# Counting the slots of a mixture of experts on TensorE, and moving one combining add to ScalarE and GpSimd, in a four-layer kernel

## The chip, the core and the metric

The kernel runs on one core of one Trainium2 chip. The metric is the device time of one execution in microseconds (us). The engines are called PE (TensorE), DVE (VectorE), ACT (ScalarE), POOL (GpSimd) and SP (SyncE), as in the profile.

## The reference

The input x is 32 sequences of 64 rows of 512 numbers, 2048 rows in all. Four layers follow one another, each of the form x = x + f(cond(x)). Only the first two matter here.

```python
x = x + L0_ffn(L0_cond(x, ...))      # attention, one shared expert, 7 routed experts of which each row takes 2
x = x + L1_ffn(L1_cond(x, ...))      # 32 routed experts of which each row takes 4
x = x + L2_ffn(L2_cond(x, ...))      # soft mixture of 16 experts
x = x + L3_ffn(L3_cond(x, ...))      # attention over a block cache, int8 product
# a routed layer:
topk, idx = top_k(x @ router, K)
y = sum over the K chosen experts e of  weight[e] * expert_e(x)
```

All is in single precision (fp32), except where small whole numbers are handled.

## The kernel before

**Tiling.** The rows are cut into 16 tiles (`NT`) of 128 rows, one row for each partition. A routed layer (class `Moe`, once with E0 = 7 experts, K0 = 2 choices and C0 = 640 slots an expert, once with E1 = 32, K1 = 4 and C1 = 320) works in three parts.

1. *Routing*, tile by tile. `choose` takes the logits of a tile and leaves the best values and their indices (`max`, `max_index`). `put` gives each chosen (row, expert) pair a slot, for n tiles at a time. It makes one-hot rows `hot` (n x K x E numbers a partition), sums them over K into `sel`, and keeps running sums over the tiles in `pre`, whose first entry holds each expert's first slot, e x C, divided by 128. Two matrix products into the PSUM tile `at` give each row the number of pairs ahead of it: a matrix of ones times `pre` adds over the 128 rows of all earlier tiles, and a strictly upper triangular matrix times `sel` adds over the earlier rows of the same tile. `hot` times `at`, summed over the experts, is the slot. `mark` then writes the row numbers into a table by slot: two comparisons on DVE make 16-bit one-hot matrices `a_` and `b_`, ACT scales `a_` by the row number, PE multiplies them, and DVE adds the product to `tokens`. After the last tile `end` casts it to `stok`, and compares the totals with C.
2. *Experts*. `ready` and `rows_of` gather the rows by `stok` with an indirect DMA issued from POOL (`xr`), and `run` multiplies unit by unit of 320 slots. The results go to the scratch tensor `ys`.
3. *Combining*, done by the layer that follows. `combined` gathers a row's K results (`yk`, an indirect DMA from POOL) and adds each, times its weight `gates`, to x with one DVE instruction. Layer 1 combines the two results of layer 0 in this way, layer 2 the four of layer 1.

**Layer 0's front** is class `Front`: thirteen stages in an order written out by hand (`turns`), four tiles in flight. Every second step `down` calls `put` for two tiles, the last two are counted in `gate_up`. `at` is a slice of the PSUM bank that `tok` and the router's logits also use.

**Layer 1's front** is the loop over 16 tiles in `layer1`: combine into `x1in`, multiply by the condition's weights on PE (`mm`), copy to `c` on ACT, write `c` to `rows` with a DMA from SP, transpose on PE (`tp`), copy to `cT` on ACT, multiply by the router on PE (`rp`), add its bias on DVE (`lg`), and choose. `put` is called for tiles 0 to 3, 4 to 7, 8 to 11, 12 and 13, 14, and 15, each one tile late. Here `at` has a bank of its own.

**Order.** Each engine runs its instructions in the order in which they stand in its queue. A scheduler makes that order, by dependences and expected times, except for those that `keep_in_program_order` pins; nothing in the parts changed here is pinned. An engine waits at the head of its queue, so what stands behind waits too.

The lines that the change and the prediction touch:

- L284 `gather`: every indirect DMA on POOL (`yk`, `xr`)
- L743 `hot`, L748 `sel`, L750 `pre`, L753 and L754 the two products, L755 `hot` times `at`, L757 its sum `sl`
- L719 the comparisons of `mark`, L725 ACT's scaling of `a_`, L727 PE's products, L728 the sum `tokens`
- L767 `stok`, L772 and L773 the totals
- L970 the combining add, L1056 `mm`, L1058 `c`, L1064 `cT`, L1067 `rp`, L1069 `lg`

`yk` has six buffers in layer 1, so a gather waits until the add of three tiles before has read its buffer.

Of the kernel before, what the change touches and what calls it, by code (L numbers as in the profile page):

```python
# [9 lines left out]
F32 = mybir.dt.float32  # L10
BF16 = mybir.dt.bfloat16
# [3 lines left out]
AF = mybir.ActivationFunctionType  # L15
ALU = mybir.AluOpType
AX = mybir.AxisListType
# [3 lines left out]
P = 128  # L21
B, T, D = 32, 64, 512
NT = B * T // P
# [5 lines left out]
E0, K0, C0, V0 = 7, 2, 640, 24  # L29
# [151 lines left out]
class Prog:  # L181


    def __init__(self, tc, a, ctx):
        self.tc, self.nc, self.a = tc, tc.nc, a
        self.const = ctx.enter_context(tc.tile_pool(name="const", bufs=1))
        self.dram = ctx.enter_context(tc.tile_pool(name="scratch", bufs=1, space=DRAM))
        self.named = {}
        self.constants(self.const, "cst")
        self.flip = 0  # L190
        self.ident = self.c("ident")
        self.ones = self.c("ones")
# [470 lines left out]
class Moe:  # L663
# [7 lines left out]
    def __init__(self, g, ctx, keep, E, K, C, V, wname, wlen, act, scale):  # L671
        self.g, self.keep, self.E, self.K, self.C, self.V = g, keep, E, K, C, V
        self.wname, self.wlen, self.act, self.scale = wname, wlen, act, scale
        tc = g.tc
        self.tiles = E * C // P
        self.rows = g.stream(f"rows{E}")
        self.ys = g.ys[E]
        self.slot = g.const.tile([P, NT, K], I32, name=f"slot{E}")
        self.gates = g.const.tile([P, NT, K], F32, name=f"gates{E}")
        self.vals = keep.tile([P, NT, 8], F32, name=f"vals{E}")  # L680
        self.chosen = keep.tile([P, NT, K], F32, name=f"chosen{E}")
        self.place = keep.tile([P, NT, K], F32, name=f"place{E}")
        self.idx = keep.tile([P, NT, 8], U32, name=f"idx{E}")

        self.pre = keep.tile([P, NT + 1, E], F32, name=f"pre{E}")
        self.count = keep.tile([P, E], F32, name=f"count{E}")
        self.stok = keep.tile([P, self.tiles], I32, name=f"stok{E}")
        self.wp = ctx.enter_context(tc.tile_pool(name=f"ew{E}", bufs=3, reuse_waits="tile"))
        self.wts = {}
# [8 lines left out]
    def begin(self, sb, bank, at):  # L698
        nc, iota = self.g.nc, self.g.c("iota")[:, 0 : self.E]
        self.bank, self.at = bank, at  # L700
        nc.vector.tensor_scalar(self.pre[:, 0], iota, self.C / P, None, ALU.mult)
        self.tok = sb.tile([P, self.tiles], F32, name="tokens", bufs=1)
        nc.vector.memset(self.tok, 0.0)

# [31 lines left out]
    def put(self, sb, i, n):  # L736

        g, nc, E, K, C = self.g, self.g.nc, self.E, self.K, self.C
        fi, place = self.chosen[:, i : i + n, :], self.place[:, i : i + n, :]
        nc.vector.tensor_copy(fi, self.idx[:, i : i + n, 0:K])  # L740
        shape = [P, n, K, E]
        hot = sb.tile(shape, F32, name=f"hot{n}", bufs=1)
        nc.vector.tensor_tensor(  # L743
            hot, g.c("iota")[:, 0:E].unsqueeze(1).unsqueeze(1).to_broadcast(shape),
            fi.unsqueeze(3).to_broadcast(shape), ALU.is_equal,
        )
        sel = sb.tile([P, n, E], F32, name=f"sel{n}")
        nc.vector.tensor_reduce(sel, hot.rearrange("p n k e -> p n e k"), AX.X, ALU.add)  # L748
        for j in range(n):
            nc.vector.tensor_tensor(self.pre[:, i + j + 1], self.pre[:, i + j], sel[:, j], ALU.add)  # L750

        at = self.at[:, 0 : n * E].rearrange("p (n e) -> p n e", n=n)
        nc.tensor.matmul(at, g.ones, self.pre[:, i : i + n], start=True, stop=False)  # L753
        nc.tensor.matmul(at, g.c("upper"), sel, start=False, stop=True)  # L754
        nc.vector.tensor_tensor(hot, hot, at.unsqueeze(2).to_broadcast(shape), ALU.mult)  # L755
        sl = sb.tile([P, n, K], F32, name=f"sl{n}")
        nc.vector.tensor_reduce(sl, hot, AX.X, ALU.add)  # L757
        slot = self.slot[:, i : i + n, :]
        nc.vector.tensor_copy(slot, sl)
        nc.vector.scalar_tensor_tensor(place, fi, -float(C), sl, ALU.mult, ALU.add)  # L760
        ov = sb.tile([P, n, K], F32, name=f"ov{n}")
        nc.vector.tensor_scalar(ov, place, float(C), BIG, ALU.is_ge, ALU.mult)
        self.mark(sb, self.bank[:, 0 : self.tiles], self.tok, sl, slot, ov, i, n, self.tiles)

    def end(self, sb):
        g, nc, E, C = self.g, self.g.nc, self.E, self.C
        nc.vector.tensor_copy(self.stok, self.tok)  # L767

        lim = sb.tile([P, E], F32, name="lim")
        nc.vector.tensor_scalar(lim, g.c("iota")[:, 0:E], float(C), float(C), ALU.mult, ALU.add)  # L770
        tot = self.at[:, 0:E]
        nc.tensor.matmul(tot, g.ones, self.pre[:, NT], start=True, stop=True)  # L772
        nc.vector.tensor_tensor(self.count, tot, lim, ALU.subtract)  # L773
        nc.vector.tensor_scalar(self.count, self.count, 0.0, None, ALU.max)

    def ready(self, ctx):
# [10 lines left out]
    def beyond(self):  # L787
# [10 lines left out]
        with tc.If(n > 0), ExitStack() as ctx:  # L798
# [10 lines left out]
            nc.vector.memset(zero, 0.0)  # L809
            end = sb.tile([P, E], F32, name="end")  # L810
            nc.vector.tensor_tensor_scan(end, tf, zero, 0.0, ALU.add, ALU.add)
            start = sb.tile([P, E], F32, name="start")
            nc.vector.tensor_tensor(start, end, tf, ALU.subtract)
            nc.vector.tensor_scalar(start, start, float(P), -float(self.C), ALU.mult, ALU.add)
            stok = sb.tile([P, V], I32, name="vtok")
# [61 lines left out]
    def run(self, xs, per_tile):  # L877

        g, nc, tc, E, K, C = self.g, self.g.nc, self.g.tc, self.E, self.K, self.C
        units = E * C // UNIT  # L880
        with ExitStack() as ctx:
            sb = ctx.enter_context(tc.tile_pool(name=f"es{E}", bufs=3, reuse_waits="tile"))
# [57 lines left out]
            for u in range(units):  # L940
                p = u // 2
# [20 lines left out]
        def combined(pool, i, bufs, x=None, out=None):  # L962
            if x is None:
                x = g.load_x(pool, xs, i, bufs)
            if out is None:
                out = x
            for k in range(K):
                yk = pool.tile([P, D], F32, name="yk", bufs=4 if K == K1 else 6)
                g.gather(yk, self.ys, self.slot[:, i, k : k + 1])
                nc.vector.scalar_tensor_tensor(out, yk, self.gates[:, i, k : k + 1], x, ALU.mult, ALU.add)  # L970
                x = out
            return out

# [1121 lines left out]
```

## Time and profile before

| | us |
|---|---|
| median of 3 runs | 2802.5 (2797.17 to 2808.08) |
| the profiled execution | 2786.42 |
| its span, first to last instruction | 2784.6 |
| PE busy in the span | 2567.1 (92%) |
| DVE busy | 1404.6 (50%) |
| ACT busy | 748.2 (27%) |
| POOL busy | 846.8 (30%) |

The profile is of one execution. "Busy" is the time in which an engine had an instruction at work; matmuls overlap, so that a busy PE is not PE at its peak. The stages follow each other in the span: layer 0's front up to about 422 us, its experts up to about 645, layer 1's front from 655 to 744, its experts up to about 1260, then layers 2 and 3. A row of a group reads: line, engine, operation, tile written and tiles read, shapes, count, then busy time and mean of one in ns, then the engine's idle time just before them and what ended it. A row of the timeline reads: start, duration, engine, line, operation, and in brackets the idle time before it with what ended that.

### The profile page before, as it was taken

How to read it: one execution, taken by the hardware profiler on the slowest of the kernel's cores; microseconds unless marked ns; L12 is line 12 of the kernel's file. 1: busy time of each engine (PE TensorE's matmuls, PEld its weight loads, DVE VectorE, ACT ScalarE, POOL GpSimd, SP SyncE). 2: the span in 40 equal slices, each digit the busy share in tenths (PEclk: the TensorE clock that was granted, in tenths of full speed). 3: DMA queues.
4: the chain of work that ended last, by engine and by line, in shares of the span. 5: the costliest groups of instructions: out<-in, count | busy, mean ns of one | idle time of the engine just before them, and what ended most of it. 6: DMA issues, size and time to landing. Idle time of an engine off the chain costs nothing.

```text
span 2784.6 us, 42002 instructions
## 1 busy us (share of the span) xinstructions
PE 2567.1 (92%) x16556; PEld 1640.1 (59%) x16571; DVE 1404.6 (50%) x3479; ACT 748.2 (27%) x1557; POOL 846.8 (30%) x904
## 2 busy tenths in 40 slices
PE   5999998997699999996899999999999999788878
PEld 4777765654555655654666666667666654344444
DVE  3666655734754333334455544445554416466656
ACT  2444430112211121111222222222222212354444
POOL 2222114624222223213122222222222108656550
PEclk9999999998699999998999999999999999889898
DMA  2233224446545965534010000001000025124340
GB/s 93 91 124 127 96 77 164 156 148 191 169 166 195 345 228 211 201 125 156 17 38 27 28 27 28 27 31 50 27 27 27 31 78 182 53 74 115 89 112 29
DMA packets 107078, 291.21 MB, mean 105 GB/s; under 512 B 20682, under 2 KB 21482, under 8 KB 99569
## 3 DMA queue, kind: packets, MB, share of 16 engines
q1 hardware_dynamic: 71232, 193.46, 19.5%
q0 software_dynamic: 35056, 89.13, 11.0%
q10 hardware_dynamic: 576, 5.77, 0.5%
q8 instruction: 135, 2.21, 0.3%
q14 instruction: 79, 0.64, 0.1%
HBM read 216.76 MB, written 87.56 MB: 109 GB/s over the span
## 4 chain that ended last, share of the span: by engine, by line
PE 48%; DVE 3%; issue 2%; POOL 1%; DMA 1%; another core or an unknown queue 1%; ACT 0%; SPq 0%; ACTq 0%; POOLq 0%; DVEq 0%
PE lp L1356 8%; PE out L1499 8%; PE zp L1433 8%; PE hp L1465 3%; PE gp L1488 2%; PE pp L1803 2%; PE y L2032 2%; PE op L2010 2%; PE sp L1963 2%; PE yp L1301 2%; PE pT L1985 2%; PE ep L1442 1%; PE kp L1936 1%; PE ap L1289 1%; PE csum L1452 1%
## 5 line engine op out<-in xcount | busy, mean ns | idle before, releaser
L910 PE MATMUL gu<-xT,wt 128*128 128x320 f32 x1472 | 407.1, 434 | 0.0
L910 PEld LDWEIGHTS gu<-xT,wt 128*128 128x128 f32 x1472 | 277.7, 191 | 119.5 <-issue 11.4
L1356 PEld LDWEIGHTS lp<-xnT,sb_mu 128*128 128x128 f32 x2048 | 235.7, 193 | 8.8 <-issue 6.7
L1356 PE MATMUL lp<-xnT,sb_mu 128*128 128x128 f32 x2048 | 238.6, 277 | 1.5 <-DVE xnT L256 0.8
L929 PE MATMUL y<-wt,hT 128*128 128x512 f32 (+1 forms) x552 | 238.7, 606 | 0.1
L1499 PE MATMUL out<-sb_w,gT 128*128 128x512 f32 x512 | 233.6, 599 | 0.0
L1433 PE MATMUL zp<-sb_w,xnT 128*128 128x512 f32 x512 | 226.5, 592 | 0.0
L1492 DVE COPY gT<-gp 128x512 f32<-128x512 f32 x64 | 44.3, 692 | 235.4 <-PE gp L1488 235.0
L284 POOL DMA_INDIRECT xr<-rows,stok x115 | 110.2, 958 | 154.7 <-PE tp L891 86.1
L1433 PEld LDWEIGHTS zp<-sb_w,xnT 128*128 128x128 f32 x512 | 93.7, 190 | 104.7 <-issue 100.9
L1499 PEld LDWEIGHTS out<-sb_w,gT 128*128 128x128 f32 x512 | 93.4, 190 | 103.5 <-issue 95.2
L929 PEld LDWEIGHTS y<-wt,hT 128*128 128x128 f32 (+1 forms) x552 | 80.0, 171 | 104.9 <-issue 88.4
L659 POOL TENSOR_TENSOR ga<-ga,sg 128x320 f32<-128x320 f32 x64 | 55.2, 863 | 283.4 <-ACT sg L655 281.3
L284 POOL DMA_INDIRECT yk<-ys,slot x96 | 99.5, 1036 | 123.9 <-SPq L798 65.2
L1510 POOL TENSOR_TENSOR xt<-xt,bc_bias 128x512 f32<-128x512 f32 x16 | 20.3, 1270 | 360.1 <-DMA x<-xt 360.1
L1470 ACT ACTIVATE h<-hp 128x512 f32<-128x512 f32 x128 | 69.5, 594 | 214.2 <-PE hp L1465 214.0
L1970 DVE CUSTOM_DVE_ANT_0 s<-sp,mask 128x336 f32<-128x336 f32 x128 | 61.4, 504 | 124.2 <-PE sp L1963 42.8
L284 POOL DMA_INDIRECT kvt<-kv,gidx x96 | 94.9, 989 | 93.6 <-PE op L2010 64.7
L1394 POOL TENSOR_TENSOR eT<-eT,inv 128x512 f32<-128x512 f32 x64 | 71.6, 1120 | 151.2 <-DVE inv L1393 149.3
L284 POOL DMA_INDIRECT kvt<-newkv,oidx x96 | 98.3, 1024 | 38.9 <-issue 29.9
L2032 PE MATMUL y<-sb_w_o,oT 128*128 128x512 f32 x128 | 74.4, 667 | 22.5 <-DVE y3s L1516 16.0
L891 PEld LDWEIGHTS tp<-sb_cst,xr 128*128 128x128 f32 x460 | 53.7, 147 | 65.4 <-issue 32.3
(379 smaller groups left out, 4616.2 us busy)
## 6 DMA issues: line engine op xcount, KB each, us to landing
wt<-w_e SPq DMA_DIRECT2D x32, 1538.0 KB
ys<-yo SPq DMA_DIRECT2D x115, 256.0 KB
ys<-zero SPq DMA_DIRECT2D x10, 2048.0 KB
xt<-x SPq DMA_DIRECT2D x62, 256.0 KB
wt<-w_e SPq DMA_DIRECT2D x7, 1536.0 KB
x<-xt SPq DMA_DIRECT2D x32, 256.0 KB
sb_w<-w SPq DMA_DIRECT2D x5, 1024.0 KB
rows<-hn SPq DMA_DIRECT2D x16, 256.0 KB
```

The lines of the kernel that those rows point to most:

```text
L284: ins = self.nc.gpsimd.indirect_dma_start(out=out, out_offset=None, in_=src, in_offset=bass.IndirectOffsetOnAxis(ap=idx, axis=0), **kw)
L910: nc.tensor.matmul(o, wj[:, c, ic * P : (ic + 1) * P], xT[:, c, :], start=c == 0, stop=c == 3)
L929: nc.tensor.matmul(y[row : row + n, :], hTs[u][:, ic, col : col + n], wd[:, ic, :], start=ic == 0, stop=ic == 1,)
L1301: g.first(c, nc.tensor.matmul(yp, self.xT[:, c, :], w["w_2"][:, c, :], start=c == 0, stop=False))
L1356: g.first(e + c, nc.tensor.matmul(lp[:, e, :], w["mu"][:, c, (4 * q + e) * P : (4 * q + e + 1) * P], self.xnT[:, c, :], start=c == 0, stop ...
L1394: g.pin(nc.gpsimd.tensor_tensor(e3, e3, inv.unsqueeze(2).to_broadcast([P, 8, T]), ALU.mult))
L1433: g.first(c, nc.tensor.matmul(zp, self.xnT[:, c, :], w["w1"][:, c, cols], start=c == 0, stop=c == 3))
L1465: g.first(e + b, nc.tensor.matmul(hp[:, b, e, :], self.ews[q][r, e, :], self.z[q][r, e * P : (e + 1) * P], start=True, stop=True))
L1470: g.pin(nc.scalar.activation(self.hs[q][b], hp[:, b], AF.Gelu))
L1499: g.first(e, nc.tensor.matmul(self.out, self.gTs[q][:, e, :], w["w2"][:, 4 * q + e, :], start=q + e == 0, stop=q + e == 6 and q == 3))
L1970: nc.vector.tensor_tensor_reduce(p, sps[j], self.masks[2 * i + half], -0.0625, 3.0e38, ALU.add, ALU.min, m)
L2032: nc.tensor.matmul(yp, self.oT[i][:, c // 2, c % 2, :], w["w_o3"][:, c, :], start=c == 0, stop=c == 3)
```

## The change

In `put`, the sums move from DVE to PE. The one-hot rows `hot` are written in bfloat16, and so are two copies of the triangular and the all-ones matrix (`masks`). `sel` and `pre` are gone. The counts in `at` are built up by 1 + K + nK products: the running base of each expert, in single precision by the identity; the triangular matrix times `hot`, for each of the K choices; and the all-ones matrix times the `hot` of each tile and choice, added to all later tiles of the call and to one further column group. ACT copies that last group to `base`, where the next call begins. The product of `hot` and `at` goes to a tile of its own, `own`. `end` takes the totals from `base` and needs no product for them.

In `combined`, for K0 = 2 choices (layer 0's results, combined in layer 1), the first add stays one DVE instruction. The second becomes two: ACT scales `yk` by the weight in place, and POOL adds it to the tile.

```diff
@@ class Moe, __init__ and begin
-        self.pre = keep.tile([P, NT + 1, E], F32, name=f"pre{E}")
+        self.base = keep.tile([P, E], F32, name=f"base{E}")
+        self.masks = keep.tile([P, 2, P], BF16, name=f"masks{E}")
...
-        nc.vector.tensor_scalar(self.pre[:, 0], iota, self.C / P, None, ALU.mult)
+        nc.vector.tensor_scalar(self.base, iota, float(self.C), None, ALU.mult)
+        for j, k in enumerate(("upper", "ones")):
+            nc.vector.tensor_copy(self.masks[:, j], self.g.c(k))
@@ put
-        hot = sb.tile(shape, F32, name=f"hot{n}", bufs=1)
+        hot = sb.tile(shape, BF16, name=f"hot{n}", bufs=1)
...
-        sel = sb.tile([P, n, E], F32, name=f"sel{n}")
-        nc.vector.tensor_reduce(sel, hot.rearrange("p n k e -> p n e k"), AX.X, ALU.add)
+        at = self.at[:, 0 : (n + 1) * E].rearrange("p (n e) -> p n e", n=n + 1)
+        nc.tensor.matmul(
+            at, g.ident, self.base.unsqueeze(1).to_broadcast([P, n + 1, E]), start=True, stop=False
+        )
+        for k in range(K):
+            nc.tensor.matmul(at[:, 0:n], self.masks[:, 0], hot[:, :, k], start=False, stop=False)
         for j in range(n):
-            nc.vector.tensor_tensor(self.pre[:, i + j + 1], self.pre[:, i + j], sel[:, j], ALU.add)
-        at = self.at[:, 0 : n * E].rearrange("p (n e) -> p n e", n=n)
-        nc.tensor.matmul(at, g.ones, self.pre[:, i : i + n], start=True, stop=False)
-        nc.tensor.matmul(at, g.c("upper"), sel, start=False, stop=True)
-        nc.vector.tensor_tensor(hot, hot, at.unsqueeze(2).to_broadcast(shape), ALU.mult)
+            for k in range(K):
+                nc.tensor.matmul(
+                    at[:, j + 1 :], self.masks[:, 1], hot[:, j : j + 1, k].to_broadcast([P, n - j, E]),
+                    start=False, stop=j == n - 1 and k == K - 1,
+                )
+        nc.scalar.copy(self.base, at[:, n])
+        own = sb.tile(shape, F32, name=f"own{n}", bufs=1)
+        nc.vector.tensor_tensor(own, hot, at[:, 0:n].unsqueeze(2).to_broadcast(shape), ALU.mult)
         sl = sb.tile([P, n, K], F32, name=f"sl{n}")
-        nc.vector.tensor_reduce(sl, hot, AX.X, ALU.add)
+        nc.vector.tensor_reduce(sl, own, AX.X, ALU.add)
@@ end
-        tot = self.at[:, 0:E]
-        nc.tensor.matmul(tot, g.ones, self.pre[:, NT], start=True, stop=True)
-        nc.vector.tensor_tensor(self.count, tot, lim, ALU.subtract)
+        nc.vector.tensor_tensor(self.count, self.base, lim, ALU.subtract)
@@ run, combined
-                nc.vector.scalar_tensor_tensor(out, yk, self.gates[:, i, k : k + 1], x, ALU.mult, ALU.add)
+                gate = self.gates[:, i, k : k + 1]
+                if K == K0 and k:
+                    nc.scalar.activation(yk, yk, AF.Copy, scale=gate)
+                    nc.gpsimd.tensor_tensor(out, out, yk, ALU.add)
+                else:
+                    nc.vector.scalar_tensor_tensor(out, yk, gate, x, ALU.mult, ALU.add)
```

## The prediction

> **What bounds the kernel now.** I read the page first, then busy time by stage, then the groups and the timeline of the one stage where both edits do most of their work.
>
> ```profile
> span 2784.6 us, 42002 instructions
> PE 2567.1 (92%) x16556; PEld 1640.1 (59%) x16571; DVE 1404.6 (50%) x3479; ACT 748.2 (27%) x1557; POOL 846.8 (30%) x904
> ```
>
> Over the whole span TensorE (PE) is the bound. The stage table (columns: stretch, its length, busy time of PE, weight loads, VectorE, ScalarE, GpSimd, then granted clock, DMA share, GB/s) shows where it is not:
>
> ```profile
> 100.00:400.00 300.00, 287.38 (x3192) 217.91 (x3191) 189.26 (x485) 121.54 (x210) 61.69 (x87) 1.00 0.31 105
> 655.00:683.00 28.00, 16.17 (x51) 9.97 (x52) 10.88 (x22) 4.62 (x9) 20.36 (x19) 0.62 0.73 212
> 683.00:714.00 31.00, 26.68 (x158) 18.91 (x157) 27.00 (x91) 12.55 (x24) 14.78 (x13) 0.87 0.63 188
> 714.00:744.00 30.00, 17.53 (x108) 13.55 (x107) 25.97 (x101) 10.22 (x19) 0.00 (x0) 0.58 0.48 190
> 755.00:1260.00 505.00, 495.27 (x1757) 286.98 (x1756) 199.16 (x410) 90.60 (x191) 126.63 (x137) 1.00 0.59 208
> ```
>
> Layer 0's front (100 to 400) and layer 1's experts (from 755) are PE at 96 to 98%. Between 655 and 744 lies layer 1's front: PE is at half clock much of the time and VectorE is busy for 53 of the 61 us after 683. GpSimd (POOL) issues 32 gathers up to 710 and then nothing. The groups of 655 to 744:
>
> ```profile
> L284 POOL DMA_INDIRECT yk<-ys,slot x32 | 35.2, 1099 | 85.7 <-SPq L798 65.2 <-DVE vals L733 10.5 <-issue 5.8
> L970 DVE SCALAR_TENSOR_TENSOR x1in<-yk,gates,x1in 128x512 f32<-128x512 f32 x16 | 11.9, 744 | 3.0 <-DMA yk<-ys,slot 2.8
> L748 DVE TENSOR_REDUCE sel<-hot 128x128 f32<-128x512 f32 x3 | 3.1, 1028 | 0.0
> L750 DVE TENSOR_TENSOR pre<-pre,sel 128x32 f32<-128x32 f32 x16 | 2.9, 184 | 0.0
> ```
>
> The last three are what the change takes from VectorE. The end of the front, in order of time:
>
> ```profile
> 722.45 0.69 DVE L755 TENSOR_TENSOR hot<-hot,at 128x512 f32<-128x512 f32 x1 [0.55 <-PE at L754]
> 724.24 0.74 DVE L970 SCALAR_TENSOR_TENSOR x1in<-yk,gates,x1in 128x512 f32<-128x512 f32 x1
> 729.19 0.59 ACT L1064 COPY cT<-tp 128x512 f32<-128x512 f32 x1 [1.26 <-PE tp L1062]
> 731.78 0.19 DVE L1069 TENSOR_TENSOR lg<-rp,bc_b_r 128x32 f32<-128x32 f32 x1 [1.23 <-PE rp L1067]
> 744.43 0.94 POOL L284 DMA_INDIRECT xr<-rows,stok  x1 [33.79 <-DVE stok L767]
> ```
>
> The last tile's second add is at 724.2, its logits at 731.8; the slots are final at 743.7, and only then can the expert rows be gathered (744.4). All that follows, PE-bound, moves with that moment.
>
> **What the Trainium skill says.** (1) "SBUF — State Buffer", Who interferes with whom: a VectorE instruction with two SBUF inputs and a GpSimd one that reads SBUF lock each other out for a whole instruction. No overlap in this trace isolates it; L1394's GpSimd multiplies do spread from 1.03 to 1.49 us. (2) "GPSIMD Engine Reference", Elementwise — side-by-side cycle accounting: a two-input add is about twice as slow there. The trace agrees: 1.27 us (L574, 128x512) against 0.74 for L970. (3) "ScalarE: Activation LUTs", What ACT_TABLE_LOAD costs: 0.83 ns an element plus a fixed part that grows by 93 ns for each per-row operand. The plain 128x512 copy is 0.59 us in the trace, so the scaled one is estimated at 0.65. (4) "TensorE: Matmul & The Clock Gate", Back-to-back issue gap: about 81 ns for a load and matmul of 128 columns. The trace agrees: 16 half-precision pairs in 1.30 us (L727 at 718.6).
>
> **The change part by part.** The sum is against the profiled execution, 2786.4 us (span 2784.6 and 1.8 around it), which is 16 below the median 2802.5 of the runs; I add the same microseconds to the median.
>
> Layer 0, eight counts of two tiles. Removed from PE: two single-precision products, four issues 0.11 us apart (112.41 to 112.74), 0.44. Added: one of them (0.22) and six 16-bit pairs at 0.08 (0.48), 0.70. So 8 x 0.26 = 2.1, minus the final total's pair (L772, 0.3): **+1.8** on a PE that is 96% busy. Ends: 0 if it all falls into PE's 4% of idling, +3. From VectorE go 0.18 + 2 x 0.18 us a count (L748, L750), worth nothing beside the busy PE. The ScalarE copy of the running base (about 0.25) is hidden likewise; the two mask copies run before the stage.
>
> Layer 1's adds. VectorE loses 16 x 0.74 = 11.9 us. ScalarE gets 16 x 0.65 = 10.4 on top of 27.4 in 89, but in its in-order queue, where each scaled copy waits for a gather to land. Behind it stand the copies `c` and `cT` (who waits: PE, then VectorE's logits) and the base copies. GpSimd gets 16 x 1.27 = 20.3 us in the queue that issues the gathers. Walk it: six gathers at 1.25 each from 655 end at 662.5. Then 26 gathers x 1.25 and 16 adds x 1.4 (1.27 and 0.13 of dispatch, estimated) are 54.9: 717.4 if it never waits. The last gather then issues at 714.8, lands 4.0 later (the first one: 654.97 to 659.07), is scaled by 719.4 and added by 720.8. That is about 4 us before the old 725.0. GpSimd, which had 13 us of waits to spare, is now the bound of this part.
>
> Layer 1's counts. VectorE loses sel (3.1 + 0.6 + 0.7) and pre (2.9): 7.3 us. PE gains 88 16-bit pairs less 7 single-precision pairs, some 5 us of a PE that is one third idle here. The new dependence is the point. In the built instruction order the multiply of hot and counts (old L755) waits for ScalarE's copy of the new base, and this copy sits in ScalarE's queue where the order puts it: for tiles 8 to 11, behind the last tile's `cT`. Walk the end: add 720.8; product 1.1 and `c` 0.6 give 722.5; ScalarE's next four instructions scale the token marks of tiles 4 to 7 (1.92): 724.4; `cT` at 725.0. From 724.1 PE works through 16 token and 20 count pairs, interleaved, 36 x 0.09 = 3.2: 727.4. Base copy 727.7. So the multiply for tiles 8 to 11 starts at 727.9, where it was 722.45. From there the old kernel took 743.5 - 722.45 = 21.0 us to the slots. Of that 2.1 us (sel, pre and the last add, by their spacing) is gone, and 1.2 of waiting for the last logits. New waits are these logits again (1.0), 12 pairs, base copy and hop for tiles 12 and 13 (0.9), the base copy behind tile 14's marks (0.5), and one hop for each base copy (1.2). 727.9 + 21.4 = 749.3: **+5.8**.
>
> The port. During 662 to 721 GpSimd adds hold it for about 20 of 59 us, and VectorE's two-input work (L970's first adds 12, the comparisons of L719 about 8, L743 2) for 22. If an add meets such work in one case of three and loses half of it (0.4 for an add, 1.1 for a 2.29 us comparison), that is about **+3**; ends 0 and +12 (every add losing 0.75). SyncE's queue gets no more and no fewer transfers; its writes of `rows` follow `c`, the expert weights behind them, and both are landed by 744. PE's clock, 0.58 to 0.87 here, may rise with more matmuls: -2 to 0, taken as 0.
>
> Sum: 1.8 + 5.8 + 3 = +10.6: 2797 for the profiled execution, **2813** on the median (+0.38%). About 0.5%, 14 us, is what a measurement of this kernel can tell from no change.
>
> **Rivals.** *GpSimd locks up the gathers (slower).* In-order adds waiting for the port delay the gathers behind them, hence the scaled copies, hence the base copies and VectorE. With adds at 1.9 and gathers at 1.5 (1.4 to 1.5 was seen on the old gathers beside L970), the queue takes 26 x 1.5 + 16 x 1.9 = 69.4 instead of 54.9: +14.5 on 1.8 + 5.8, about 2825. It passes 0.5% once adds average 1.8 us. For it: GpSimd becomes the bound with no slack; against it: the order keeps three tiles of gathers ahead. *VectorE's relief decides (faster).* VectorE is 87% busy after 683. If queue positions on ScalarE don't bind, half of the moved adds (6) and all of sel and pre (7.3) come off: -13.3 + 1.8 is -11.5, 2791; over 0.5% only if the early adds count too (-17, 2785). Against it: the walk finds ScalarE, not VectorE, last. *No effect:* the moved scaling could load a table each time (1.28 us). Between plain copies and L725's scaled ones the stage shows no load before 736.8, so I exclude it.
>
> **How the numbers follow.** The walk 0.60, mostly -3 to +18; the GpSimd lock 0.30, +14 to +30; VectorE's relief 0.10, -17 to -6. Within 0.5%: about 0.42 of the first, 0.05 of the second, 0.07 of the third, and the rest of the first lies above 14. I give 0.05 faster, 0.55 same, 0.40 slower. The range leaves out the top of the lock and the bottom of the relief: 2793 to 2832.
>
> **What would show it.** Right: no L748/L750 groups; GpSimd adds of 1.3 to 1.6 us between gathers up to about 720 to 725; the multiply for tiles 8 to 11 waiting for ScalarE at 726 to 730, after the last `cT`; first xr gather at 748 to 755; layer 0 ending 1 to 2 us later. Wrong: that gather before 744 (relief won), or after 758 with adds near 2 us (lock), or a layer 0 shifted by over 4 us.

## The result, and the profile after

The changed kernel takes 2814.73 us (median of 20 runs) beside 2804.76 us for the kernel before (20 runs): ratio 1.0034, 95% interval [1.0018, 1.0049], about 9.5 us more by the ratio. The profiled execution of it took 2813.8 us, the one of before 2786.4, which is less than the fastest of the 20 runs (2792.84). Most of that gap of 27 us is scatter: up to layer 3 the traces are only some 7 us apart, and the other 20 come up in layer 3, whose code the change doesn't touch (502 us before, 522 after, and 506 in a second trace of the same changed kernel).

In all that follows, "the stretch" is layer 1's front from the first `yk` gather to the cast of the slots to integers (`stok`). It was 88.5 us before (654.97 to 743.49) and is 91.2 us after (656.82 to 748.03). The head of the page:

```profile
span 2812.0 us, 42199 instructions
PE 2586.5 (92%) x16660; PEld 1648.7 (59%) x16675; DVE 1392.4 (50%) x3421; ACT 760.6 (27%) x1587; POOL 864.5 (31%) x920
```

VectorE (DVE) lost 12 us over the whole span and GpSimd (POOL) gained 18. The stage table, columns as before, shows where it went:

```profile
655.00:683.00 28.00, 15.03 (x54) 9.03 (x54) 7.01 (x20) 8.82 (x15) 22.21 (x22) 0.62 0.60 177
683.00:714.00 31.00, 28.41 (x163) 20.96 (x161) 18.33 (x55) 13.99 (x27) 26.24 (x22) 0.70 0.61 183
714.00:744.00 30.00, 18.99 (x168) 14.93 (x168) 26.91 (x83) 14.81 (x31) 8.59 (x6) 0.81 0.61 229
```

In the first two rows VectorE fell from 37.9 to 25.3 us of 59, and GpSimd rose from 35.1 to 48.5. The engine that had time to spare is now the full one. The groups of 655 to 744, shapes kept apart:

```profile
L284 POOL DMA_INDIRECT yk<-ys,slot x32 | 33.2, 1037 | 73.8 <-SPq L806 65.3 <-issue 5.4 <-DVE own L765 1.3
...
L982 POOL TENSOR_TENSOR x1in<-x1in,yk 128x512 f32<-128x512 f32 x16 | 23.9, 1492 | 3.7 <-ACT yk L981 3.3 <-issue 0.2
...
L984 DVE SCALAR_TENSOR_TENSOR x1in<-yk,gates,xt 128x512 f32<-128x512 f32 x16 | 13.6, 849 | 22.1 <-DMA yk<-ys,slot 22.1
L981 ACT ACTIVATE yk<-yk,gates 128x512 f32<-128x512 f32 x16 | 11.6, 722 | 25.5 <-DMA yk<-ys,slot 24.0 <-POOL x1in L982 1.5
...
L722 DVE TENSOR_TENSOR a<-sb_cst,tl 128x1280 f16<-128x1280 f32 x3 | 6.6, 2197 | 0.0
```

Two of these groups looked like this in the kernel before:

```profile
L970 DVE SCALAR_TENSOR_TENSOR x1in<-yk,gates,xt 128x512 f32<-128x512 f32 x16 | 11.9, 744 | 9.7 <-DMA yk<-ys,slot 9.7
L719 DVE TENSOR_TENSOR a<-sb_cst,tl 128x1280 f16<-128x1280 f32 x3 | 4.5, 1485 | 0.0
```

Two things are to be seen. GpSimd's own queue hardly waits: apart from the wait before the first gather (65.3) its gathers waited 8.5 us and its adds 3.7, where the old gathers waited 20.5. And three means are too high for what the instructions do. The GpSimd add averages 1.49 us although 14 of the 16 took 1.26 to 1.29; VectorE's first add averages 0.85 (15 took 0.73 to 0.75 and one 2.43), where the kernel before had 0.74; the comparison `a` of 1280 columns averages 2.20, where each of before's took 1.48. The end of the stretch, in order of time:

```profile
723.34 2.66 POOL L982 TENSOR_TENSOR x1in<-x1in,yk 128x512 f32<-128x512 f32 x1 [1.97 <-ACT yk L981]
726.06 1.12 PE L1070 MATMUL mm<-x1in,wbd 128*128 128x512 f32 x2 [1.61 <-POOL x1in L982]
727.70 1.92 ACT L728 ACTIVATE a<-a,sb_cst 128x320 f16<-128x320 f16 x4
729.52 0.57 ACT L1078 COPY cT<-tp 128x512 f32<-128x512 f32 x1
730.76 0.18 ACT L763 COPY base<-at 128x32 f32<-128x32 f32 x1 [0.67 <-PE at L759]
730.98 0.69 DVE L765 TENSOR_TENSOR own<-hot,at 128x512 f32<-128x512 bf16 x1
731.67 0.19 DVE L1083 TENSOR_TENSOR lg<-rp,bc_b_r 128x32 f32<-128x32 f32 x1
749.06 0.96 POOL L284 DMA_INDIRECT xr<-rows,stok  x1 [23.06 <-DVE gm L1112]
```

The last add takes 2.66 us, and TensorE waits for it. Behind the last tile's product stand, in TensorE's queue, that tile's transposes, another tile's logits, and then the token products and the counts of tiles 8 to 11; after these come the base copy and the multiply (L765), which starts at 730.98, where it was 722.45. This is the chain that the prediction walked, but for `cT`, which the counts don't wait for. The last logits (731.67) are where they were (731.78). The expert gather comes at 749.06 instead of 744.43. From that gather to the start of the experts' last product it is 509.2 us, 508.1 before: the experts only move.

### The profile page after: what moved, and what is told of

The parts are those of the page before. It is cut to its first block, busy times and chain, and to the rows that moved or that the text cites. A ratio compares the mean times of both kernels' runs of the same rounds, so it can differ in the third digit from the quotient of the medians.

```text
span 2812.0 us, 42199 instructions
## 1 busy us (share of the span) xinstructions
PE 2586.5 (92%) x16660; PEld 1648.7 (59%) x16675; DVE 1392.4 (50%) x3421; ACT 760.6 (27%) x1587; POOL 864.5 (31%) x920
## 3 DMA queue, kind: packets, MB, share of 16 engines
q0 software_dynamic: 35056, 89.13, 10.6%
## 4 chain that ended last, share of the span: by engine, by line
PE 47%; DVE 3%; another core or an unknown queue 2%; issue 1%; POOL 1%; ACT 1%; DMA 1%; POOLq 0%; ACTq 0%; SPq 0%; DVEq 0%
PE out L1513 8%; PE lp L1370 8%; PE zp L1447 7%; PE hp L1479 3%; PE gp L1502 2%; PE pp L1817 2%; PE y L2046 2%; PE sp L1977 2%; PE op L2024 2%; PE yp L1315 2%; PE pT L1999 2%; PE ep L1456 1%; PE kp L1950 1%; PE ap L1303 1%
## 5 line engine op out<-in xcount | busy, mean ns | idle before, releaser
L284 POOL DMA_INDIRECT yk<-ys,slot x96 | 97.6, 1017 | 112.9 <-SPq L806 65.3
L284 POOL DMA_INDIRECT kvt<-kv,gidx x96 | 93.3, 972 | 122.4 <-PE op L2024 95.7
L1988 ACT ACTIVATE s<-s,m 128x336 f32<-128x336 f32 x128 | 73.1, 574 | 80.5 <-DVE m L1984 41.1
```

Source lines behind the costliest of these rows:

```text
L284: ins = self.nc.gpsimd.indirect_dma_start(out=out, out_offset=None, in_=src, in_offset=bass.IndirectOffsetOnAxis(ap=idx, axis=0), **kw)
L1988: nc.scalar.activation(p, p, AF.Exp, bias=m, scale=-1.0, accum_out=tot)
```

## The experiments

Runs of one group shared a chip and the runs of the kernel before that belong to it; medians of before were 2792.5, 2704.6 and 2791.7 us for the three groups, so ratios are compared and not microseconds.

### Group 1: the parts alone

**adds**: only the last hunk of the change, the scaled copy on ScalarE and the sum on GpSimd; its diff is that hunk:

```diff
-                nc.vector.scalar_tensor_tensor(out, yk, self.gates[:, i, k : k + 1], x, ALU.mult, ALU.add)
+                gate = self.gates[:, i, k : k + 1]
+                if K == K0 and k:
+                    nc.scalar.activation(yk, yk, AF.Copy, scale=gate)
+                    nc.gpsimd.tensor_tensor(out, out, yk, ALU.add)
+                else:
+                    nc.vector.scalar_tensor_tensor(out, yk, gate, x, ALU.mult, ALU.add)
```

> Of the change, the moved add of layer 1 alone; counting as before. T1 (the moved add paces layer 1's front: the GpSimd order, and VectorE's two-input comparisons and GpSimd's adds blocking each other): first yk gather to first xr gather 92 to 95 us (89.5 before, 92.2 with the whole change), a GpSimd add of 2.5 us or more and a VectorE comparison of 2.5 us where they overlap, median 2808 to 2812. T2 (the counts' chain TensorE, ScalarE, VectorE paces it): front 89 to 90 us, median within 3 us of before. Both: layer 0's stok cast stays at 421.3 us.

Measured: ratio 1.0038 [1.0021, 1.0056]; stretch 98.8 us, longer than either theory had it.

**counts**: all hunks but that one.

```diff
-                if K == K0 and k:
-                    nc.scalar.activation(yk, yk, AF.Copy, scale=gate)
-                    nc.gpsimd.tensor_tensor(out, out, yk, ALU.add)
-                else:
-                    nc.vector.scalar_tensor_tensor(out, yk, gate, x, ALU.mult, ALU.add)
+                nc.vector.scalar_tensor_tensor(out, yk, gate, x, ALU.mult, ALU.add)
```

> Of the change, the counts on TensorE alone (both layers); the second add of layer 1 as before on VectorE. T1: layer 0 ends 1 to 2 us later as with the whole change (stok cast 422.5), layer 1's front takes 89.5 us or less (down to 86, since the stretch from the last large multiply to the cast was 17.1 us against 21.0), median between 3 us under and 2 us over before. T2: front 92 to 93 us as with the whole change, median 2811 to 2815.

Measured: 0.9985 [0.9974, 0.9997]; stretch 84.5 us.

**counts1** and **counts0** choose the counting by the layer (counts1 as shown; in counts0 it is `E == E0`); the first branch holds the new lines of `put`, the second the old ones:

```diff
+        self.on_pe = E == E1
...
+        if self.on_pe:
...
+        else:
+            sel = sb.tile([P, n, E], F32, name=f"sel{n}")
+            nc.vector.tensor_reduce(sel, hot.rearrange("p n k e -> p n e k"), AX.X, ALU.add)
...
```

> Of the change, the counts on TensorE in layer 1 alone; layer 0's counts and layer 1's adds as before. T1: stok cast of layer 0 at 421.3, front 86 to 89.5 us, median 0 to 5 us under before: a kernel that could beat both. T2: front 92 to 93 us, median 3 to 5 us over before.

> Of the change, the counts on TensorE in layer 0 alone. T0 (the counting products lie on TensorE's path in layer 0): stok cast 1 to 1.5 us and first yk gather 1.2 to 2.5 us later than before (421.3, 655.0), front of layer 1 as before (89.5), median 1 to 3 us over before. Against it (the later cast of layer 0 is scatter): both within 0.5 us of before, median the same.

Measured: counts1 0.9988 [0.9975, 1.0001], stretch 83.9 us; counts0 1.0008 [0.9992, 1.0025], stretch 87.8 us.

So the two halves of the change have opposite signs: alone, the moved add costs 0.4%, and the counts gain some 0.15%. In the kernel with the add alone the GpSimd queue, cut from the timeline of that engine, looks like this near its end:

```profile
717.57 1.79 POOL L974 TENSOR_TENSOR x1in<-x1in,yk 128x512 f32<-128x512 f32 x1 [0.23 <-DVE pre L750]
719.51 0.97 POOL L284 DMA_INDIRECT yk<-ys,slot  x1
720.49 1.28 POOL L974 TENSOR_TENSOR x1in<-x1in,yk 128x512 f32<-128x512 f32 x1
...
724.45 3.17 POOL L974 TENSOR_TENSOR x1in<-x1in,yk 128x512 f32<-128x512 f32 x1
737.70 1.26 POOL L974 TENSOR_TENSOR x1in<-x1in,yk 128x512 f32<-128x512 f32 x1 [10.07 <-DVE pre L750]
```

The last sum waited 10 us for VectorE: in this kernel's order the last tile's first add (the other half of the pair) stands behind the old counting, L750 among it, on VectorE. In the whole change the last tile's first add starts at 721.65, before the last counts, and the stretch is 91.2. So in the traces the moved add and the old counts collide. The runs don't show this: the whole change came to 1.0034 and, in group 3, 1.0037, no better than `adds` with 1.0038, and a plain sum of the halves (0.38 - 0.15 = 0.23%) lies within the intervals too.

With the counts alone the end of the stretch reads (timeline of VectorE):

```profile
726.01 0.68 DVE L765 TENSOR_TENSOR own<-hot,at 128x512 f32<-128x512 bf16 x1
...
743.33 0.20 DVE L777 CAST stok<-tokens 128x80 int32<-128x80 f32 x1
```

From the multiply of tiles 8 to 11 to the cast it takes 17.3 us, in counts1 also 17.3, and in the whole change 17.1; before it took 21.0, and in counts0, whose layer 1 is as before, also 21.0. This is the gain of the counts. About half of it is work: VectorE was busy for 17.6 us of this part before and for 15.7 in counts. The rest is waits, and TensorE's granted clock may have a share in these: it was 0.50 in this part in the three traces with the old counts (before, counts0, adds) and 0.59 to 0.71 in the others. No run takes the two apart. The multiply itself starts 67.2 and 66.6 us into the stretch, as before (67.5): on its way there the new chain costs nothing that can be seen.

For layer 0 one trace doesn't settle it. From the first tile's logits to the last tile's, the four kernels with the old counts there took 337.6, 341.6, 338.9 and 339.8 us (mean 339.5), and the ten with the new ones, all groups together, 336.9 to 343.9 (mean 339.8). The runs don't settle it either: counts and counts1 differ by layer 0 alone, and came to 0.9985 and 0.9988.

### Group 2: what makes the moved add dear

**iota_psum**: the comparisons of layer 1 read their counting row from PSUM.

```diff
@@ begin
+        self.iota = g_iota = self.g.c("iota")
+        if self.E == E1:
+            self.iota = at[:, 384:512]
+            nc.vector.tensor_copy(self.iota, g_iota[:, 0:P])
@@ mark
-    def mark(self, sb, ps, tok, sl, slot, ov, i, n, tiles):
+    def mark(self, sb, ps, tok, sl, slot, ov, i, n, tiles, iota=None):
...
+        iota = self.g.c("iota") if iota is None else iota
@@ put
-        self.mark(sb, self.bank[:, 0 : self.tiles], self.tok, sl, slot, ov, i, n, self.tiles)
+        self.mark(sb, self.bank[:, 0 : self.tiles], self.tok, sl, slot, ov, i, n, self.tiles, self.iota)
```

> The whole change, and layer 1's large comparisons (the marks of slot row and slot tile) read their counting row from PSUM instead of SBUF, so that a GpSimd add and a comparison don't both want the shared access to SBUF. Lock theory (the moved add costs because the two engines block each other there): no mark of tile over 1.6 us and no GpSimd add over 1.4 us while a comparison runs, against 2.55 and up to 3.36; first yk gather to stok cast 87 to 89 us against 91.2; ratio to before 1.000 to 1.003. Order theory (it costs because gathers stand behind adds that wait for earlier steps in GpSimd's queue): durations may fall, the stretch stays at 90.5 to 92.5 us and the ratio at 1.003 to 1.005.

Measured: 1.0030 [1.0022, 1.0039]. All three `a` took 1.48 to 1.49 us and no GpSimd add over 1.31. The multiply of tiles 8 to 11 started 70.4 us into the stretch (74.2 with the whole change), but from there to the cast it took 23.0 us and the stretch came to 93.3. The waits of TensorE in the end of the stretch (us in total, times, the longest) say what was late instead:

```profile
PE tok L735 <- DVE b L727: 12.7, 3, 5.3
PE tok L735 <- ACT a L733: 3.1, 1, 3.1
```

In this kernel the multiply of tiles 12 and 13 started at 735.28, after both comparisons of tiles 8 to 11 (728.94 to 732.63); in the whole change it was before them. The row shares a PSUM tile with the counts, and that seems to put them in this order. A second run of the idea follows in group 3.

**sum_dve**: the scaled copy stays on ScalarE, the plain sum is VectorE's.

```diff
-                    nc.gpsimd.tensor_tensor(out, out, yk, ALU.add)
+                    nc.vector.tensor_tensor(out, out, yk, ALU.add)
```

> The whole change, but the plain sum after ScalarE's scaled copy on VectorE instead of GpSimd. If GpSimd (its order or the blocking) makes the moved add dear: first yk gather to stok cast 84 to 86 us (84.5 without the moved add), ratio 0.997 to 1.000. If the extra hop through ScalarE makes it dear (0.72 us scaled copy, ScalarE's queue): 89 to 92 us, ratio 1.002 to 1.004.

Measured: 1.0019 [1.0010, 1.0027]; stretch 89.1 us. GpSimd then only issues gathers, no `a` takes over 1.49, and still the stretch is 4.6 us longer than with the counts alone. GpSimd's timeline near the end of the gathers, and VectorE's comparisons at that time:

```profile
693.38 4.46 POOL L284 DMA_INDIRECT yk<-ys,slot  x1 [2.31 <-issue]
706.64 1.43 POOL L284 DMA_INDIRECT yk<-ys,slot  x1 [8.81 <-DVE idx L737]
...
716.48 0.96 POOL L284 DMA_INDIRECT yk<-ys,slot  x1 [4.73 <-DVE chosen L743]
```

```profile
693.32 2.29 DVE L722 TENSOR_TENSOR b<-sb_cst,row 128x2048 f16<-128x2048 f32 x1
695.53 1.49 DVE L722 TENSOR_TENSOR a<-sb_cst,tl 128x1280 f16<-128x1280 f32 x1
...
707.25 2.28 DVE L722 TENSOR_TENSOR b<-sb_cst,row 128x2048 f16<-128x2048 f32 x1
709.45 1.48 DVE L722 TENSOR_TENSOR a<-sb_cst,tl 128x1280 f16<-128x1280 f32 x1
```

So one instruction split in two over two engines cost 0.19% without any sum on GpSimd. Two gathers took 4.46 and 3.37 us to issue instead of 0.95, and both began while a comparison was running and ended 0.82 us after the end of the pair: the blocking needs no GpSimd add. That is 5.9 us more in GpSimd's queue, and the last gather was issued 63.1 us into the stretch, 55.8 with the counts alone. The long waits for VectorE (8.8 and 4.7 us) are no mark of this kernel, since with the counts alone the gathers waited for VectorE about as long (8.9 us once, 5.6 in three more). A second reading is that a `yk` buffer is held longer while its tile waits for ScalarE and then for VectorE. How the loss divides between the long issues and the held buffers wasn't tested.

**base_dve** and **counts_bdve**: the running total copied by VectorE, in the whole change and with the old add.

```diff
-        nc.scalar.copy(self.base, at[:, n])
+        nc.vector.tensor_copy(self.base, at[:, n])
```

> The whole change, but the running total is copied out of PSUM by VectorE instead of ScalarE. The prediction's step (the multiply waits for the copy in ScalarE's queue): the multiply of tiles 8 to 11 starts 1 to 3 us earlier, first yk gather to stok cast 88 to 90 us against 91.2. The trace's reading (the copy waited for the count products on TensorE, not for ScalarE): the stretch stays within 1 us of 91.2, and only the hop of some 0.2 us per group of tiles goes.

> The counts on TensorE in both layers, the adds as before, and the running total copied by VectorE: the version that might beat both kernels. If the hop through ScalarE costs in every group of tiles: 0.2 to 1.5 us less per layer than with ScalarE's copy (first yk gather to stok cast 83 to 84.5 us against 84.5; ratio 0.997 to 0.9985). If nothing waits for that copy: the same as without it, 0.9985. If VectorE is what fills the stretch: the added VectorE copies (0.2 us each) make it 84.5 to 85.5.

Measured: base_dve 1.0028 [1.0016, 1.0040], stretch 92.1 us, multiply of tiles 8 to 11 at 74.8 us into it (74.2 with ScalarE's copy). VectorE's timeline there:

```profile
730.05 0.19 DVE L763 COPY base<-at 128x32 f32<-128x32 f32 x1 [0.27 <-PE at L759]
730.16 0.68 DVE L765 TENSOR_TENSOR own<-hot,at 128x512 f32<-128x512 bf16 x1
```

The copy waits for TensorE's counts here too. So ScalarE's queue was not what the multiply stood behind. counts_bdve: 0.9976 [0.9961, 0.9991], stretch 79.6 us, which looked like a better version; group 3 tries it further.

### Group 3: the blocking again, the scatter, and a better version

**iota_tok**: as iota_psum, with one word changed.

```diff
-            self.iota = at[:, 384:512]
+            self.iota = bank[:, 384:512]
```

> As the run with the counting row in PSUM, but in the bank of the token sums instead of the counts' bank: there the large multiply of tiles 8 to 11 started 3.8 us earlier than with the whole change (70.4 after 74.2 us from the first yk gather), and the rest up to the stok cast took 23.0 us against 17.1. If sharing the counts' bank ordered the next group's counts behind the comparisons (it ate the gain): multiply again at 69 to 71, rest 17 to 20, stretch 86.5 to 90.5 us, ratio 1.001 to 1.003. If the blocking at SBUF was worth nothing: stretch at 91 to 94 us again, ratio 1.003 or more.

Measured: 1.0015 [1.0005, 1.0026]; stretch 89.0 us; multiply of tiles 8 to 11 at 72.3 us, then 16.7 us to the cast.

**again**: the changed kernel, unedited.

> The whole change once more, unedited, for the scatter of one trace: stretch from first yk gather to stok cast 91.2 us within 1 us (two kernels with the same layer 1 gave 88.5 and 87.9, two others 84.5 and 83.9), ratio 1.002 to 1.005. If the stretch moves by 3 us or more, single traces of it tell nothing of this size.

Measured: 1.0037 [1.0024, 1.0051]; stretch 91.4 us. The stretch repeats within 0.3 us, and iota_tok, on the same chip, is 2.5 us shorter in it. In the medians of their runs they differ by 5.9 us (2801.5 and 2795.6). The query by tile on iota_tok's GpSimd adds (durations are minimum, median and maximum in ns):

```profile
L987 POOL TENSOR_TENSOR x1in<-x1in,yk x16: 1267/1275/1285, 666.3 to 724.7; 128x512 f32<-128x512 f32 x16
its engine sat idle before it (us, times) until:
  ACT yk L986: 5.1, 1
```

and the groups of VectorE in its stretch:

```profile
L989 DVE SCALAR_TENSOR_TENSOR x1in<-yk,gates,xt 128x512 f32<-128x512 f32 x16 | 13.6, 848 | 23.1 <-DMA yk<-ys,slot 23.0
L727 DVE TENSOR_TENSOR b<-tok,row 128x2048 f16<-128x2048 f32 x3 | 6.8, 2279 | 0.0
L727 DVE TENSOR_TENSOR a<-tok,tl 128x1280 f16<-128x1280 f32 x3 | 4.4, 1478 | 0.0
```

Minimum, median and maximum of the add are now one number (1.267, 1.275, 1.285 us), and `a` is back at 1.48 us each. VectorE's first adds, which still read two tiles from SBUF, still average 0.85, as one of them took 2.31 beside the GpSimd add at 691.67. So the blocking between a GpSimd add and a VectorE instruction with two SBUF operands is real, and it goes where one operand comes from PSUM. Part of the moved add's price stays: 1.0015 against 0.9985 with the counts alone, and 89.0 against 84.5 us in the stretch.

**counts1_bdve** and **best_yk7**: layer 1's counts alone with VectorE's copy; and counts_bdve with one buffer more for `yk` (the diff shows that edit).

```diff
-                yk = pool.tile([P, D], F32, name="yk", bufs=4 if K == K1 else 6)
+                yk = pool.tile([P, D], F32, name="yk", bufs=4 if K == K1 else 7)
```

> The counts on TensorE in layer 1 alone, running total copied by VectorE, layer 0 and the adds as before. If layer 0's counts cost 1 to 2 us (the prediction's step): ratio 0.9970 to 0.9976, under the 0.9976 of the run with both layers. If they cost nothing: 0.9976 within 0.0007. Stretch of layer 1: 79 to 81 us (79.6).

> The counts on TensorE in both layers, running total copied by VectorE, adds as before, and 7 instead of 6 buffers for yk in layer 1. If the buffers hold the gathers back (6.4 us in one wait for VectorE): stretch 77 to 79 us, ratio 0.9965 to 0.9975. If the last groups of tiles set the end and not the gathers: 79 to 80.5 us, ratio 0.9976.

Measured: counts1_bdve 0.9994 [0.9980, 1.0008], stretch 86.3 us; best_yk7 1.0015 [1.0003, 1.0028], stretch 91.6 us. Both missed what was expected. The three kernels with VectorE's copy and the old add took 79.6, 86.3 and 91.6 us for nearly the same code. The stage table from 660 to 695 (columns as above), first for counts_bdve:

```profile
660.00:695.00 35.00, 25.64 (x149) 17.67 (x150) 20.51 (x61) 10.75 (x19) 26.94 (x26) 0.84 0.85 258
```

and for best_yk7:

```profile
660.00:695.00 35.00, 18.40 (x50) 11.15 (x51) 11.04 (x30) 3.96 (x8) 18.03 (x19) 0.51 0.56 168
```

TensorE's granted clock was 0.84 in the one and 0.51 in the other, and all engines got through less. The two windows don't lie alike, since the first gather was issued at 658.63 and at 663.47. Over 36 us from the first gather the clock was 0.83 in counts_bdve and 0.52 in best_yk7; counts1_bdve had 0.73 and the other kernels with the old add (before, counts, counts0, counts1) 0.68 to 0.71. In best_yk7 the clock stood at 0.50 all the way from 661 to 698, in counts_bdve it was at 1.00 from 671.2 to 698. With it VectorE waited longer for TensorE's logits: 22.4 us in best_yk7, 2.9 in counts_bdve. That the clock is the cause, and not the buffer or another order of instructions, is argued and not shown. A low clock in one trace alone isn't the answer either, since the runs rank the three kernels as the traces do (0.9976, 0.9994, 1.0015). With the moved add the stretch did not follow the clock: 91.2 us at 0.59, 91.4 at 0.73 and, in base_dve, 92.1 at 0.83, over the same 36 us.

What does not depend on the start of the stretch is the rest after the multiply of tiles 8 to 11: 19.7, 19.8 and 19.6 us with VectorE's copy and the old add, 17.3 twice with ScalarE's. VectorE stood 1.0 us in one of its copies there for TensorE's counts (counts_bdve, counts1_bdve). But base_dve, with VectorE's copy and the moved add, took 17.2, so the copy alone is not shown to be the reason, and it stays on ScalarE for want of a gain.

The version to keep is counts: 0.15% under the kernel before, interval 0.03% to 0.26%. It beats both kernels, by little. The 0.9976 of counts_bdve, from ten runs on another chip, was not repeated.

## Why the prediction was right, and where it was not

The forecast, +10.6 us and a change too small to tell at 0.5%, held: +9.5 and +10.3 us by the two ratios (0.0034 x 2804.8 and 0.0037 x 2791.7). Its steps held less well than their sum.

- **The GpSimd walk: mechanism and time right.** Predicted: last add ends 65.8 us after the first gather (720.8 - 655.0). In iota_tok, where nothing blocks an add, it ends at 66.9 (724.7 + 1.3 - 659.1). GpSimd, which had spare time, became the engine that this part waits for. That its queue is the whole price is not shown: sum_dve has no adds in it and lost 0.19%.
- **The port: real, and within its range.** Predicted +3, in the range 0 to +12. In the whole change the 16 adds took 23.9 us, in iota_tok 20.4: 3.5 us more on GpSimd. The last add ends at 69.2 instead of 66.9, and the stretch is 2.3 to 2.5 us longer than iota_tok's; in the runs the difference is 5.9 us. The Trainium skill, "SBUF — State Buffer", Who interferes with whom, says that a VectorE instruction with at most one SBUF input doesn't contend with GpSimd, outside the modes in which it uses two ports, while one with two SBUF inputs does; these traces agree, with `a` at 2.55 and 1.48 us.
- **The scaled copy: too small.** Estimated 0.65 us, measured 0.72. The fixed part and the price for a per-row operand that the Trainium skill, "ScalarE: Activation LUTs", What ACT_TABLE_LOAD costs, gives would have made 0.186 + 0.093 + 512 x 0.000833 = 0.706 (an estimate); I had added only part of it to the plain copy's duration.
- **The chain from the last add to the multiply: too long by 2.** Predicted 7.1 us (720.8 to 727.9), measured 5.0 (726.00 to 730.98). The 36 pairs of token and count products were put at 3.2 us and ran from 729.16 to 730.73, 1.6 us, or 44 ns a pair. The 81 ns that the prediction read from the old trace (16 pairs in 1.30 us) were measured at a granted clock of 0.50, and with 80 columns; here the clock was 1.00. The named waiter was wrong as well: the base copy was said to stand behind `cT` in ScalarE's queue, but `cT` ended at 730.09 and the copy waited 0.67 more for the counts on TensorE. Moving the copy to VectorE (base_dve) brought the multiply no earlier.
- **From the multiply to the slots: the step that failed.** Predicted 21.4 us, measured 17.1, and 17.3 with the counts alone. The 3.3 us taken off (counting and the wait for the last logits) were right, and 21.0 - 3.3 is 17.7. The 3.6 us of new waits put on top were not there: between that multiply and the cast VectorE waited 1.2 us for the last token products, as before, and 0.3 us once for ScalarE, and for nothing else that the profile shows. In the whole change the multiply of tiles 12 and 13 started at 732.76, right behind other VectorE work and after its base copy (732.54 to 732.73), with no wait shown.
- **Layer 0: not resolved.** Predicted +1.8; counts0 gives 1.0008 [0.9992, 1.0025], which holds 0 and 1.8 us alike, and the traces' means differ by 0.3 us with a scatter of 6.
- **The sum.** Predicted for layer 1's front: 5.8 + 3 = 8.8 us. The traces show 2.7 (91.2 - 88.5), 2.9 with the second trace. That leaves some 7 us of the measured 9.5 to 10.3 without a place. An unlucky trace of before doesn't explain it, since counts0, with the same layer 1, took 87.8 us. Against the mean of these two (88.2), the seven kernels that lack either the scaled copy or layer 1's new counts changed their stretch as they changed their runs, within 3 us (adds +10.6 and +10.6, counts -3.6 and -4.2, best_yk7 +3.4 and +4.2). The six that have both lost 3 to 7 us more in their runs than in their stretch. No run here tells where, so it stays open. The forecast put nearly all of its sum into layer 1's front, where the traces show a third of it: part of its closeness is luck.

Of the rivals, *the GpSimd lock* happened at a fraction of its size: adds averaged 1.49 us, not 1.9, and its gathers 1.04, not 1.5. *VectorE's relief* is real only for the counts: alone they give 4.0 us in the stretch. The adds' relief was worth nothing, since VectorE waited for gathers and for GpSimd instead: its remaining adds idled 22.1 us for `yk`, where both adds of before together idled 12.7 (9.7 and 3.0).

## What to carry to other kernels

Before moving work to an engine because it is idle on average, walk its queue in the stage that matters: GpSimd was 30% busy overall, but in this stage it issues the gathers that everything waits for, and 20 us of adds filled that queue. Splitting one fused instruction over two engines cost time even where the second engine is fast (sum_dve). Look at where a gather's issue lands, too: begun beside a long comparison it took two to five times as long. A price read from a trace holds for the clock of that moment: note the clock beside it. When two edits come together, run them apart: here one, alone, was a gain of 0.15%, the other a loss of 0.4%.

## What the runs showed of the hardware that I had not expected

- The blocking takes in small instructions too, and gathers: in the whole change a shift of 16 integers per row (L713) took 1.15 and 1.89 us instead of 0.17, one of VectorE's adds 2.43 instead of 0.75, and one gather's issue 2.04 instead of 0.95 us. A comparison of 2048 columns took 4.03 us instead of 2.28 in the run with the add alone.
- For the gathers it takes no GpSimd add. In the kernels whose counting row is in SBUF, seven gathers came to their issue while a comparison of 1280 or 2048 columns was running (one each in after, again and base_dve, two each in adds and sum_dve). Each of the seven ended 0.82 or 0.84 us after the end of a comparison, and six of them took 2.04 to 4.46 us. With the row in PSUM five gathers came to their issue so (iota_psum, iota_tok), and took 0.95 to 0.97. In before and in counts no gather met a comparison. One issue of 2.11 us in counts1 met none of these comparisons, but a one-hot comparison of 512 columns (`hot`), and ended 0.82 us after its end as well.
- Moving one operand of the comparisons to PSUM cost nothing: 2.28 us for 2048 columns and 1.48 for 1280, as from SBUF.
- TensorE's granted clock over the first 36 us of the gathers, where TensorE is busy for 55 to 72% of the time, ranged from 0.52 to 0.83 over traces of nearly the same work. It is a mean of stretches at 0.50 and at 1.00; the first one at 0.50 lasted to about 671 in counts_bdve and to 698 in best_yk7.
